# Weight loads four ahead, seven early units, and a later first stage in a fused attention and convolution kernel

## Chip, cores and metric

The kernel runs on one NeuronCore of one Trainium2 chip. The metric is the device time of one execution in microseconds (us), in float32 throughout. Its engines are named as the profile names them: PE (matrix multiply), PEld (its weight loads), DVE (vector), ACT (scalar), POOL (GpSimd) and SP (sync, used here only to issue DMAs).

## The reference

Two layers run one after the other on x of shape (2, 256, 64, 64).

```
# layer 0: global attention, 8 heads of 32 channels over all 4096 positions of an image
m    = resize(mask, bilinear)
q, k, v = 1x1 convolutions of x;  q = q / sqrt(32)
fuse = softmax(q k^T) v
x    = conv1x1(concat[x, fuse], Wf) * m + x * (1 - m)

# layer 1: channel gate, window attention, two grouped 7x7 convolutions
x = x * sigmoid(relu(x ca_w1) ca_w2)
x = x + window_attention(x)          # 8x8 windows, 4 heads of 64
x = channel shuffle(x)
y = relu(bn1(grouped conv7x7(x, sa_w1)))
y = bn2(grouped conv7x7(y, sa_w2))
out = x * sigmoid(y)
```

## The kernel before

**Preparation** (to about 187 us of the span): q, k and v of both images are projected and stored in DRAM, and the mask and the scaled convolution taps are prepared.

**Attention.** The 4096 queries of an image are cut into 8 chunks of 512, so there are 16 chunks (b, c). A chunk has 64 *slots*: 2 groups of 4 heads (g) by 32 key blocks of 128 (m). The slots of all chunks stand in one list, 1024 long, and one loop issues them in that order. In iteration i it issues the scores of slot i + 2 (L633 on PE, exponentials L643 on ACT into a tile e), then the products of slot i (L662 on PE, which read e and v), and the addition of e to the running sum of exponentials (L664 on DVE). The e tiles come from a ring of EB = 8 buffers. A buffer is free again once its product and its addition are done.

**Work put between slots.** `at(delay, action)` runs an action `delay` iterations later. After a chunk's last slot (slot 63 of the first chunk) come, with DN = 8: at + 8 the denominators (matmuls L685, copy L692 to the tile inv); at + 9 their reciprocal (L714 on DVE); at + 10 and + 12 the two halves of `spread` (matmuls L700 with inv as an operand, copy L707 to the tile rd); at + 13 the multiplication of the attention output f by rd (L717 on DVE); and at + 14 the chunk's *stage* is queued. A stage is a generator. The loop advances it by one step in every fourth iteration. Its first step multiplies x and then f by the fusion weights (L732), and its DVE part makes x1 (L744, L746). The following steps are the channel gate (L761, L775), the window attention (L803 to L953), and the storing of the chunk's rows to the DRAM tensor x_s (L979). [...]

**The last part** is the pair of grouped convolutions, `convolve`, also a generator. A *unit* u is 16 of the 256 channels' group work with its own banded weights w_s[u] (896 KB), 16 units in all. `items` lists the pieces of work: the first EARLY units of image 0 alone, the units 2 to EARLY - 1 of image 1 alone, the other units for both images together, and the units 1 and 0 of image 1. Image 1 is complete only when the last chunk's stage has stored its rows. So the first EARLY items run between the steps of that last stage, and fill PE there. For item k, `conv1(k)` is L1045 (56 matmuls), `conv2(k)` is L1069 (56 matmuls), and `gate(k)` multiplies (L1091) and stores the result (L1104). `load_x` (L1024) loads an item's rows from x_s: into four tiles "xe" for k < EARLY and four tiles "xl" after that. `load_w` (L1017) loads a unit's weights. Those of unit 0 have a tile of their own. The others go into the eight e buffers of the attention, in turn, and the order of loads is 1 to 15 and then 1 again. Both kinds of load are issued on SP's queue, where half of the stores stand too (for the early items after the last stage, all stores go to POOL).

The order around the last stage comes from this code:

```
            for _ in range(2):
                load_w(weights.popleft())
            conv1(0)
...
                gate(k, z)
                if xcs or k + 4 < EARLY:
                    load_rows(k + 4)

                if weights and (k < EARLY - 1 or k >= EARLY):
                    load_w(weights.popleft())
```

`more()` (L1110) makes the four xl tiles as soon as the last stage has been issued, and loads the next four items' rows into them.

Of the kernel before, what the change touches and what calls it, by code (L numbers as in the profile page):

```python
# [29 lines left out]
AHEAD = 2  # L30
EB = 8
DN = 8
EARLY = 8
HEADS1, HD1 = 4, 64
WS = 8
NW = W // WS
# [19 lines left out]
def conv_seq_kernel(ctx: ExitStack, tc: tile.TileContext, a, out):  # L56
    nc = tc.nc
# [13 lines left out]
    def psum2(name):  # L71
        return ps["pair"].tile([P, 2, CH], F32, tag="s", name=name)
# [259 lines left out]
    def spread(row, n):  # L332
        f = row.shape[-1]
        return row.rearrange("p u f -> u p f").to_broadcast([NU, n, f])
# [189 lines left out]
    def pipeline(arm, shifted, pools):  # L524
# [23 lines left out]
        stages = deque()  # L548

        def at(delay, action):  # L550
            later.append((now[0] + delay, action))
# [13 lines left out]
        def load_q(b, c):  # L565
            q = qp.tile([P, KC, CH], F32, tag="q", name=f"q{arm}_{b}_{c}")
            nc.sync.dma_start(q, q_s[b, c].rearrange("p (g n) -> p g n", g=KC))
            qts[b, c] = q
# [82 lines left out]
        def products(i):  # L651
            b, c, g, m = slots[i]
            if m == 0:
                acc[0] = avp.tile([P, CH], F32, tag="av", name=f"av{arm}_{i}")
                acc[1] = ep.tile([P, HG, CH], F32, tag="sum", name=f"sum{arm}_{i}", bufs=3)
                totals[b, c, g] = acc[1]
            av, total = acc[0], acc[1]
            e, v = es[i], vts[b, c, g, m // PB]
            start, stop = m == 0, m == NMB - 1
            for j in range(HG):  # L660
                r = slice(32 * j, 32 * j + 32)
                nc.tensor.matmul(av[r, :], v[:, m % PB, r], e[:, j, :], start=start, stop=stop)  # L662
            if m > 0:
                nc.vector.tensor_add(total, first[0] if m == 1 else total, e)  # L664
            e = es.pop(i)
            if start:
                first[0] = e
            if stop:
                if g == 0:
                    fts[b, c] = fp.tile([P, KC, CH], F32, tag="f", name=f"f{arm}_{b}_{c}")  # L670
                f = fts[b, c]
                nc.scalar.copy(f[:, g, :], av)  # L672
                if g == 0:
                    return
                both = [totals.pop((b, c, gg)) for gg in range(KC)]
                inv = fp.tile([P, P], F32, tag="inv", name=f"inv{arm}_{i}")
                rd = fp.tile([P, KC, 4, P], F32, tag="rd", name=f"rd{arm}_{i}")


                def denominators():  # L680
                    s = psum2(f"dn{arm}_{i}")
                    for h in range(HEADS0):
                        for q in range(4):
                            r = slice(32 * q, 32 * q + 32)
                            nc.tensor.matmul(  # L685
                                s[r, 0, 0:P],
                                keysum[:, h].rearrange("p i h -> p (i h)"),
                                both[h // HG][:, h % HG, q * P : (q + 1) * P],
                                start=(h == 0),
                                stop=(h == HEADS0 - 1),  # L690
                            )
                    nc.scalar.copy(inv, s[:, 0, 0:P])  # L692


                def spread(hh):
                    t = psum2(f"rd{arm}_{i}_{hh}")
                    for gg in range(KC):
                        for q in range(2):
                            r = slice(64 * hh + 32 * q, 64 * hh + 32 * q + 32)
                            nc.tensor.matmul(  # L700
                                t[:, q, gg * P : gg * P + P],
                                spread_h[r, gg].rearrange("p j d -> p (j d)"),
                                inv[r, :],
                                start=True,
                                stop=True,
                            )
                    nc.scalar.copy(  # L707
                        rd[:, :, 2 * hh : 2 * hh + 2, :],
                        t[:, :, 0 : KC * P].rearrange("p q (g n) -> p g q n", g=KC),
                    )  # L710


                at(DN, denominators)
                at(DN + 1, lambda: nc.vector.reciprocal(inv, inv))  # L714
                at(DN + 2, lambda: spread(0))
                at(DN + 4, lambda: spread(1))
                at(DN + 5, lambda: nc.vector.tensor_mul(f, f, rd.rearrange("p g q n -> p g (q n)")))  # L717

# [266 lines left out]

        items = [(u, (0,)) for u in range(EARLY)] + [(u, (1,)) for u in range(2, EARLY)]
        items += [(u, (0, 1)) for u in range(EARLY, NU)] + [(1, (1,)), (0, (1,))]
        staged = []  # L990

        def convolve():
# [12 lines left out]
            weights = deque([*range(1, NU), 1])  # L1005
            dst = out.rearrange("b (g i) r w -> b i r g w", i=4)

            def load_w(u):
                if u >= NU:
                    return  # L1010
                n = 2 * 32 * UW
                if u == 0:
                    t = cpool.tile([P, n], F32, name=f"w{arm}{u}")
                else:
                    t = ep.tile([P, HG, CH], F32, tag="e", name=f"w{arm}{u}")
                    t = t.rearrange("p h n -> p (h n)")[:, 0:n]
                nc.sync.dma_start(t, w_s[u])  # L1017
                ws[u] = t

            def load_x(k):  # L1020
                u, images = items[k]
                x = xs[k] = early[k % 4] if k < EARLY else xcs[k % 4]
                for i, b in enumerate(images):
# [5 lines left out]
            def load_rows(k):  # L1029

                while len(xs) < min(k + 1, len(items)) and (
                    staged or B - 1 not in items[len(xs)][1]
                ):
                    load_x(len(xs))
# [53 lines left out]
            def gate(k, z):  # L1088
# [5 lines left out]
                if k == len(items) - 1:  # L1094
                    engines = (nc.scalar, nc.sync)
                elif staged and k < EARLY:
                    engines = (nc.gpsimd,)
# [12 lines left out]
            def more():  # L1110
                if staged and not xcs:

                    for n in range(3):
                        t = ep.tile([P, HG, CH], F32, tag="sum", name=f"xl{arm}{n}", bufs=3)
                        t = t.rearrange("p h n -> p (h n)")[:, 0 : B * nb * UG * WP]
                        xcs.append(t.rearrange("p (n g w) -> p n g w", n=B * nb, g=UG, w=WP))
                    xcs.append(pool.tile([P, B * nb, UG, WP], F32, name=f"xl{arm}3"))
                    load_rows(EARLY + 3)
                return bool(xcs)
# [2 lines left out]
            load_rows(3)  # L1122
            load_w(0)
            pool = yield
            for _ in range(2):
                load_w(weights.popleft())
            conv1(0)
            yield
            for k, (u, images) in enumerate(items):
                while len(xs) <= k + 1 < len(items):  # L1130
                    if not more():
                        yield
                conv1(k + 1)
                yield
                more()
                z = conv2(k)
                yield
                more()
                gate(k, z)
                if xcs or k + 4 < EARLY:  # L1140
                    load_rows(k + 4)

                if weights and (k < EARLY - 1 or k >= EARLY):
                    load_w(weights.popleft())

        def run_later():
# [23 lines left out]
        for i, (b, c, g, m) in enumerate(slots):  # L1170
            now[0] = i
            if (b, c, g, m) == (B - 1, NCHUNK - 1, 0, 0):
                for _ in banded:
                    pass
                conv = convolve()
                next(conv)
            if m % PB == 0:
                load_piece(i // PB + AHEAD)
            if g == KC - 1 and m == 0:
                nxt = (b, c + 1) if c + 1 < NCHUNK else (b + 1, 0)  # L1180
                if nxt[0] < B:
                    load_q(*nxt)
            rest = scores(i + 2) if i + 2 < len(slots) else None
            products(i)
            if rest:
                rest()
            if g == KC - 1 and m == NMB - 1:
                at(DN + 6, lambda b=b, c=c: stages.append(stage(b, c)))
            run_later()
            if i % 5 == 1:  # L1190
                next(banded, None)
            if i % 4 == 0:
                run_stages()
# [102 lines left out]
```

## Time and profile before

| what | value |
|---|---|
| median of 3 runs | 3022.46 us (3018.35 to 3022.87) |
| the profiled execution | 3021.93 us, span 3020.1 us |
| mean granted PE clock | 0.993 |
| PE busy | 2970.8 us, 98% |
| DVE busy | 2503.1 us, 83% |
| ACT busy | 2480.6 us, 82% |
| POOL busy | 267.1 us, 9% |
| attention, first score matmul to last product | 187.4 to 2781 us |
| last part, to the end of the span | 2781 to 3020 us |

Busy shares are averages over stretches with different limits: the attention takes 86% of the span, and what limits the last part has to be read from its own lines. Numbers in the traces are us from the span's start, and a duration of one instruction is in ns. The profiled execution spends 1.8 us outside its span.

### The profile page before, as it was taken

Reading aid. Unit: us, or ns where it says so; the run is one execution under the profiler, and the core shown is the slowest. Engines: PE = TensorE matmul, PEld = TensorE weight load, DVE = VectorE, ACT = ScalarE, POOL = GpSimd, SP = SyncE. Lnnn points to the kernel's source line nnn. Section 1 sums busy time; section 2 is a strip of 40 time slices with the busy share of each in tenths; the row PEclk is TensorE's granted clock in tenths of the full one; section 3 lists DMA queues with packets and bytes.
Section 4 is the critical chain, followed back from the end, with each engine's and each line's share of the span. In section 5 each row is a group of like instructions: output and inputs, shape, how many; then the busy total and the mean of one; then the engine's idle time right before and its main releaser. Section 6 shows DMA issues by size and latency. Waiting matters only on the chain.

```text
span 3020.1 us, 61026 instructions
## 1 busy us (share of the span) xinstructions
PE 2970.8 (98%) x25226; PEld 1017.2 (34%) x25226; DVE 2503.1 (83%) x1348; ACT 2480.6 (82%) x4151; POOL 267.1 (9%) x470
## 2 busy tenths in 40 slices
PE   9999899999999999999999999999999999999897
PEld 3552223223222222222223222323223222323585
DVE  3249989999999999998999999999999998998211
ACT  5569789898989898988989898989898998988333
POOL 8010000000000000000000000000000000000456
PEclk9999999999999999999999999999999999999998
DMA  8544322222142323232222222222323222321564
GB/s 243 196 174 160 107 69 66 69 65 70 52 80 63 79 62 73 66 73 68 67 68 64 71 58 67 62 73 62 80 59 69 71 71 67 104 60 54 163 196 104
DMA packets 224143, 266.03 MB, mean 88 GB/s; under 512 B 113576, under 2 KB 130300, under 8 KB 223600
## 3 DMA queue, kind: packets, MB, share of 16 engines
q1 hardware_dynamic: 200880, 231.47, 26.2%
q0 software_dynamic: 18416, 27.87, 4.4%
q8 instruction: 201, 3.29, 0.5%
q10 hardware_dynamic: 4560, 2.70, 0.3%
q14 instruction: 86, 0.70, 0.1%
HBM read 213.49 MB, written 66.13 MB: 93 GB/s over the span
## 4 chain that ended last, share of the span: by engine, by line
PE 92%; DVE 2%; DMA 2%; POOL 1%; ACT 1%; issue 1%; SPq 0%; ACTq 0%; DVEq 0%; POOLq 0%
PE sa L633 36%; PE ava L662 33%; PE hya L732 4%; PE qka L803 4%; PE vwa L889 2%; PE opa L953 2%; PE v L472 2%; PE q L435 2%; PE k L435 2%; DVE suma L664 1%; POOL out_dram L1104 1%; PE c1a L1045 1%; PE c2a L1069 1%; DMA out_dram<-za 1%; PE dna L685 1%
## 5 line engine op out<-in xcount | busy, mean ns | idle before, releaser
L664 DVE TENSOR_TENSOR suma<-suma,ea 128x2048 f32<-128x2048 f32 x960 | 2199.1, 2291 | 88.7 <-ACT ea L643 2.3
L643 ACT ACTIVATE ea<-sa 128x512 f32<-128x512 f32 (+1 forms) x3072 | 2044.8, 745 | 86.6 <-PE sa L633 39.3
L633 PE MATMUL sa<-qa,ka 32*128 32x512 f32 x8192 | 1191.4, 640 | 1.5 <-ACT vst L480 1.2
L662 PE MATMUL ava<-ea,va 128*32 128x512 f32 x8192 | 1091.6, 605 | 0.3 <-ACT fa L672 0.3
L633 PEld LDWEIGHTS sa<-qa,ka 32*128 32x128 f32 x8192 | 338.0, 183 | 755.4 <-ACT ea L643 688.3
L662 PEld LDWEIGHTS ava<-ea,va 128*32 128x32 f32 x8192 | 161.5, 108 | 779.7 <-issue 752.9
L979 POOL DMA_DIRECT2D xs<-xo x94 | 65.8, 708 | 2552.0 <-DVE xo L964 2551.8
L1104 POOL DMA_DIRECT2D out_dram<-za x210 | 117.9, 569 | 85.0 <-DVE za L1091 61.1
L803 PE MATMUL qka<-ua,qkv_w 128*128 128x512 f32 x256 | 118.4, 605 | 0.0
L664 DVE TENSOR_TENSOR suma<-ea,ea 128x2048 f32<-128x2048 f32 x32 | 73.1, 2284 | 51.3 <-ACT ea L643 51.3
L1091 DVE TENSOR_TENSOR za<-za,xla 128x768 f32<-128x768 f32 (+1 forms) x16 | 21.7, 1359 | 108.0 <-DMA out_dram<-za 57.9
L454 DVE TENSOR_REDUCE top<-sq 128x512 f32<-128x2048 f32 x16 | 36.6, 2286 | 81.3 <-ACT sq L448 81.3
L1069 PE MATMUL c2a<-yca,wa 32*128 32x192 f32 (+1 forms) x1344 | 98.1, 435 | 2.5 <-ACT za L1079 2.5
L740 ACT ACTIVATE ta<-hya,bf 128x512 f32<-128x512 f32 x32 | 20.2, 683 | 96.8 <-PE hya L732 96.8
L1079 ACT ACTIVATE za<-c2a 128x384 f32<-128x384 f32 (+1 forms) x48 | 26.1, 595 | 86.5 <-DMA out_dram<-za 61.4
L1069 PEld LDWEIGHTS c2a<-yca,wa 32*128 32x128 f32 x1344 | 89.6, 315 | 13.1 <-issue 9.8
L858 ACT ACTIVATE ewa<-ewa,mxwa 128x64 f32<-128x64 f32 x256 | 85.2, 346 | 1.5 <-DVE mxwa L849 1.5
L744 DVE TENSOR_TENSOR ta<-ta,mca 128x512 f32<-128x512 f32 x32 | 22.0, 689 | 67.6 <-ACT ta L740 67.6
L816 ACT ACTIVATE qka<-qka,qkv_b 128x512 f32<-128x512 f32 x64 | 40.4, 683 | 41.8 <-PE qka L803 41.6
L803 PEld LDWEIGHTS qka<-ua,qkv_w 128*128 128x128 f32 x256 | 46.0, 189 | 71.3 <-issue 46.1
L435 PE MATMUL q<-x,WqT 128*128 128x512 f32 x128 | 61.3, 624 | 5.6 <-DMA WqT<-in_WqT_dram 5.6
L889 PE MATMUL vwa<-qkv_w,ua 128*128 128x256 f32 x256 | 59.5, 386 | 0.0
(137 smaller groups left out, 1523.5 us busy)
## 6 DMA issues: line engine op xcount, KB each, us to landing
ka<-ks SPq DMA_DIRECT2D x256, 256.0 KB
va<-vs SPq DMA_DIRECT2D x256, 256.0 KB
wa<-ws SPq DMA_DIRECT2D x17, 896.0 KB
ws<-zeros SPq DMA_DIRECT2D x16, 896.0 KB
xs<-xo POOLq DMA_DIRECT2D x78, 140.0 KB, 5.8
xla<-xs SPq DMA_DIRECT2D x24, 420.0 KB
x<-in_x_dram SPq DMA_DIRECT2D x16, 512.0 KB
qs<-qst SPq DMA_DIRECT2D x16, 512.0 KB
```

Of the source, the lines that this page charges most:

```text
L435: nc.tensor.matmul(s[:, g, :], w[:, kc, g * P : (g + 1) * P], rhs, start=(kc == 0), stop=(kc == KC - 1),)
L633: nc.tensor.matmul(heads[j], k[r, cols], q[r, g, :], start=True, stop=not shifted)
L643: nc.scalar.activation(e[:, h, :], tile, AF.Exp, scale=SCALE0)
L662: nc.tensor.matmul(av[r, :], v[:, m % PB, r], e[:, j, :], start=start, stop=stop)
L664: nc.vector.tensor_add(total, first[0] if m == 1 else total, e)
L732: nc.tensor.matmul(s[:, oc, :], wf[:, kc, oc * P : (oc + 1) * P], f[:, kc - KC, :] if half else xw[kc], start=(kc == 0), stop=(kc == 2 * K ...
L803: nc.tensor.matmul(s[:, j, :], wqkv[:, kc, o : o + P], u[:, kc, :], start=(kc == 0), stop=(kc == KC - 1),)
L858: nc.scalar.activation(e[:, n, :], e[:, n, :], AF.Exp, bias=mx[:, n : n + 1], accum_out=rs[:, n : n + 1],)
L889: nc.tensor.matmul(sv[:, t, :], u[:, kc, t * P : (t + 1) * P], wqkv[:, kc, 2 * C : 3 * C], start=(kc == 0), stop=(kc == KC - 1),)
L979: eng.dma_start(x_s[b, n, p + r0 : p + r1].rearrange("r g w -> g r w"), xo[64 * h : 64 * h + 64, oc, r0 - WS * c : r1 - WS * c, :],)
L1069: nc.tensor.matmul(tiles[j // 2][:, j % 2, 0 : n * W], w[r, d], y[r, 0:n, d : d + W], start=(d == 0), stop=(d == KS - 1),)
L1104: engines[stores % len(engines)].dma_start(dst[b, i, r0:r1, UG * u : UG * u + UG, :], z[p + r0 : p + r1, :, nb * m + n, :],)
```

## The change

Two unrelated parts.

In the first chunk only, the two halves of `spread`, the multiplication of f and the start of the stage come EB + 1 = 9 slots later; denominators and reciprocal stay where they were.

In the last part, EARLY goes from 8 to 7. Unit 7 is then done for both images together: 23 items in place of 24. Four units' weights are loaded ahead of the first convolution in place of two, and after each item the next one follows as long as its number is at most 1 + EB = 9, or once the early items are over.

```
-EARLY = 8
+EARLY = 7
...
+                late = EB + 1 if (b, c) == (0, 0) else 0
                 at(DN, denominators)
                 at(DN + 1, lambda: nc.vector.reciprocal(inv, inv))
-                at(DN + 2, lambda: spread(0))
-                at(DN + 4, lambda: spread(1))
-                at(DN + 5, lambda: nc.vector.tensor_mul(f, f, rd.rearrange("p g q n -> p g (q n)")))
+                at(DN + 2 + late, lambda: spread(0))
+                at(DN + 4 + late, lambda: spread(1))
+                at(DN + 5 + late, lambda: nc.vector.tensor_mul(f, f, rd.rearrange("p g q n -> p g (q n)")))
...
-            for _ in range(2):
+            for _ in range(4):
                 load_w(weights.popleft())
...
-                if weights and (k < EARLY - 1 or k >= EARLY):
+                if weights and (weights[0] <= 1 + EB or k >= EARLY):
                     load_w(weights.popleft())
...
-                at(DN + 6, lambda b=b, c=c: stages.append(stage(b, c)))
+                late = EB + 1 if (b, c) == (0, 0) else 0
+                at(DN + 6 + late, lambda b=b, c=c: stages.append(stage(b, c)))
```

## The prediction

> **What bounds the kernel now.** I read the waits of PE over the whole run first, then the order of time around each long wait, then the queue that stands behind it.
>
> ```profile
> PE c1a L1045 <- DMA wa<-ws: 12.5, 3, 9.4
> PE rda L700 <- issue: 9.0, 1, 9.0
> PE q L435 <- DMA WqT<-in_WqT_dram: 5.6, 1, 5.6
> ```
>
> Columns: total us, times, longest. From the first attention slot to the last part PE has one long wait, at L700; all others before the last part that fall into the attention are 1.2 us or less. In the last part it waits three times for weights at L1045. These are the two places that the change touches. In windows of one chunk's length from 378.7 to 2658.8 PE is busy without a gap, 162.86 us per chunk, while DVE is busy for about 151.3 us of it.
>
> The first wait, on PE and on DVE:
>
> ```profile
> 351.20 1.07 PE L662 MATMUL ava<-ea,va 128*32 128x512 f32 x8
> 361.26 1.01 PE L700 MATMUL rda<-inva,spread_h 32*128 32x128 f32 x6 [8.99 <-issue]
> ```
> ```profile
> 343.63 16.67 DVE L664 TENSOR_TENSOR suma<-suma,ea 128x2048 f32<-128x2048 f32 x7
> 360.21 0.94 DVE L714 RECIPROCAL inva<-inva 128x128 f32<-128x128 f32 x1
> ```
>
> Columns: start, duration, then the idle time in brackets. The first chunk has no stage to work on. PE alone needs 2.067 us for a slot, DVE 2.395 us for an addition, so PE runs ahead until the e ring is full (near 298 us) and then keeps DVE's pace. Slot 73's products end at 352.3. The spread needs the reciprocal, which stands on DVE behind the additions up to slot 72 and ends at 361.2: PE waits 9.0 us although the bracket says only "issue". In that time DVE works off all of PE's lead, and from then on PE sets the pace.
>
> The second place, PE and SP's queue:
>
> ```profile
> 2839.46 4.19 PE L1045 MATMUL c1a<-xea,wa 128*32 128x192 f32 x56 [1.84 <-DMA wa<-ws]
> ...
> 2853.20 3.58 PE L1069 MATMUL c2a<-yca,wa 32*128 32x192 f32 x56
> 2866.15 4.62 PE L1045 MATMUL c1a<-xea,wa 128*32 128x192 f32 x56 [9.38 <-DMA wa<-ws]
> 2870.70 3.58 PE L1069 MATMUL c2a<-yca,wa 32*128 32x192 f32 x56
> 2874.20 2.54 PE L1045 MATMUL c1a<-xla,wa 128*32 128x192 f32 x56
> ```
> ```profile
> 2848.76 1.33 SPq L979 DMA_DIRECT2D xs<-xo x2
> 2856.16 2.01 SPq L1024 DMA_DIRECT2D xla<-xs x4
> 2858.22 1.54 SPq L1017 DMA_DIRECT2D wa<-ws x3
> ```
>
> Unit 7's weights are issued behind four row loads, which wait until the last chunk's rows have landed in x_s. The 9.38 us are thus the price of the queue's order. Also, conv1 takes 2.47 us in a row of items, but 4.12 to 4.55 us right after the two longer waits.
>
> **What the Trainium skill says.** "TensorE: Matmul & The Clock Gate" (What's actually happening) has the PE clock fall to half after an idle window of about 3.4 us and return after a busy one. The trace agrees: granted clock 0.50 from 356 to 364 us and from 2862 to 2870, also some 4 us into the work. The same page (Architectural detail) calls DVE strict FIFO; that is the first wait. "DMA: Bandwidth & Descriptors" (Queues, rings and completion order) says that a DMA engine takes the descriptors of one ring in order and alternates between rings by packets. I use it for the first of four row loads landing first; the trace has no landing time for it.
>
> **Part 1, the later spread and stage.** It adds and removes no instruction: 16 matmuls and two copies of `spread`, one DVE multiplication, and the stage's steps with their two loads on SP (next x and mask) and four stores on POOL move by 9, the stage in effect by 8 slots (from 80 to 88, as it starts in every fourth). The loads are for a stage at slot 144, and POOL is idle for hundreds of us there, so the moved DMAs cost nothing.
>
> Slot 82 is where PE now wants the reciprocal. PE passes slot 73 at 352.3; DVE has the reciprocal at 361.2; at 2.067 us per slot PE needs 18.6 us for nine slots. So the old wait goes.
>
> What is late next? With a full ring, L662 of slot i starts 4.2 us after the addition of slot i - 8 ends (319.15 against 314.97 for slot 60). DVE has slot 73's addition done at 363.4, later ones each 2.395 us after. PE: slot 80 at 365.7 by its own pace; from slot 82 by the ring; slot 88 starts at 380.1 + 4.2 = 384.3 and ends at 385.3. The two spread halves (0.65 us each) fit into the 0.33 us that each slot leaves. The stage's first half (x, 3.53 us) ends at 388.8. Its second half needs f, whose multiplication stands on DVE behind slot 85's addition: 363.4 + 12 x 2.395 = 392.1, plus 1.22 = 393.4. **A new wait of about 4.6 us** at L732. Behind it on PE stand the scores of slot 91 on, so ACT waits as well, but DVE still has three additions. For the clock I charge 1.6 us: what the old wait cost after its end (378.65 - 361.26 = 17.4 us for seven slots and the spread, which at full clock are 14.5 + 1.3).
>
> Then 393.4 + 3.53 + 1.6, four slots (8.27) and the gate's first product (1.05) give 407.9. The wait for x1 that stands there is covered: DVE has it at 400.4 + 2.8 = 403.2. Before, the same amount of work was done at 412.66 (first L803, after slot 92) less the second gate product 1.05 = 411.6. **Gain 3.7 us.** It stays, since PE sets the pace thereafter and DVE's end at slot 137 (525.3 before, less at most the 7.4 us it idled in that chunk) is 517.9, ahead of PE's 522.0. Bounds: 5.4 without the clock loss; 7.1, what DVE's unbroken row allows; and 0, if the wait at f is as long as the old one.
>
> **Part 2, weights and units.** Weights 3 and 4 are issued when the additions of their e buffers end, at about 2772 and 2775; SP has nothing else until 2805. So the waits of 1.24 and 1.84 us go, and with the second the slow conv1 (4.12 - 2.47 = 1.65): **4.7 us**, all on PE's path through the stage. Weights 5 to 8 follow the first four gates, one per gate as now, and all stand ahead of the row loads. So the 9.38 us and the slow conv1 after them (4.55 to the next start, less 2.47: 2.1) go, **11.5 us**.
>
> Next late: with EARLY = 7 the eighth conv1 is image 1's unit 2 and needs the first of the row loads. Count from the end of the last L953 (2847.2 now). The rows' load is issued 8.95 us later (2856.16). I take 3.5 us to landing. The skill's fit for one DMA ("DMA: Bandwidth & Descriptors", Anatomy of one DMA: 2.0 us + bytes/436e3) gives the estimate 3.0 for 420 KB; the trace's longest is the 9.9 us in which all four and a weight tile landed. PE meanwhile has conv2, conv1, conv2 = 3.51 + 2.47 + 3.50 = 9.5 us. Wait: 8.95 + 3.5 - 9.5 = 3.0, plus 0.5, since weight 8 now moves while the rows are stored. With 1 us for the clock (nothing to 2.1): **4.5 us come back**; at worst 8.95 + 9.9 - 9.5 + 2 for weight 8 + 2.1 = 13.5; at best, with 3.0 to landing and no more, 2.5.
>
> Unit 7: two single items (2.47 + 3.50 each, 11.94) become one double item (4.74 + 4.89 = 9.63): **2.3 us less**. Later weights keep at least seven items' lead; they reuse buffers whose unit is done. POOL's stores (6.74 us per early item, three instead of four items) end before their z buffer is needed, and the double items leave POOL 2.9 us free in each 9.63, so the end drains as before.
>
> Sum: 4.7 + 11.5 - 4.5 + 2.3 = **14.0 us** (5 to 16). With part 1: 17.7. The profiled execution took 3021.93 (span 3020.1 and 1.8 around it), 0.5 below the median: **3004**.
>
> **Rivals.** *Part 2 alone pays* (the wait at f equals the one removed): 3008. For it: f stands on DVE behind nearly as many additions. Against: the ring limits the backlog. *The row loads take over fully* (all four land together): part 2 gives 5, with part 1 3013. For it: one ring, 0.5 us between issues. *Nothing hangs on these waits* (removed waits reappear elsewhere; the change doesn't do what it says): 3020. Against: PE has no gap between the two places. *All clear* (no clock losses, f in time): 3021.9 - 7.1 - 16 gives 2999. *Slower*: keeping DVE backlogged makes it the bound in every chunk at L700 and L732. Its chunk is 151.3 us busy plus 62 gaps of 0.1, 157; from 162.9 on it decides. At 2 us beyond, 15 chunks cost 30 and the total is 3034. Nothing shows DVE slowed by backlog.
>
> **How the numbers follow.** About 0.2% (6 us) can be told from no change. Forecast, 2999 to 3010: 0.60. Part 2 alone: 0.12, row loads: 0.12, all clear: 0.09, all faster by over 0.2% as 3016 is the border: 0.93. Nothing: 0.04. Slower: 0.03. The range 2997 to 3013 leaves out the last two and some edges.
>
> **What would show it.** After: no wait of 9 us at L700, one of 3 to 6 at L732 in the first chunk with DVE's f as its end; no L1045 wait for wa; one of 2 to 5 for xla at the eighth conv1; 23 pairs of L1045 and L1069 groups, so 112 matmuls fewer; the last L953 some 8 us earlier. Wrong, if L700 or L732 waits come back chunk after chunk, or if the wait for xla is above 10.

## The result, and the profile after

The changed kernel took 3003.48 us (median of 4 runs, 3002.89 to 3005.29) against 3022.66 us before (median of 4 runs, 3018.35 to 3024.31): ratio 0.994, 95% interval 0.9924 to 0.9955. Its profiled execution took 3003.67 us with a span of 3001.9, so the span is 18.2 us shorter. Line numbers after the edit are higher by 3 from L714 on, and in split, best5, best8 and best8_act by one more.

The waits of PE over the whole run, in the changed kernel (total us, times, longest):

```profile
PE q L435 <- DMA WqT<-in_WqT_dram: 5.6, 1, 5.6
PE hya L735 <- DVE fa L720: 4.3, 1, 4.3
PE c1a L1048 <- DMA xla<-xs: 3.8, 1, 3.8
...
PE c2a L1072 <- ACT za L1082: 0.6, 1, 0.6
```

The 9.0 us at L700 and the 12.5 us for weights are gone. Two shorter waits have come: for f in the first chunk's stage, and for the rows of image 1.

The first chunk, PE and then DVE, in order of time (start, duration, idle time before in brackets):

```profile
385.03 3.70 PE L735 MATMUL hya<-xa,WfT 128*128 128x512 f32 x8
393.01 5.40 PE L735 MATMUL hya<-fa,WfT 128*128 128x512 f32 x8 [4.29 <-DVE fa L720]
398.34 1.14 PE L633 MATMUL sa<-qa,ka 32*128 32x512 f32 x8
...
406.61 1.08 PE L764 MATMUL ca1a<-x1a,ca_w 128*64 128x256 f32 x8
```
```profile
359.98 0.95 DVE L717 RECIPROCAL inva<-inva 128x128 f32<-128x128 f32 x1
360.84 30.98 DVE L664 TENSOR_TENSOR suma<-suma,ea 128x2048 f32<-128x2048 f32 x13
391.74 1.22 DVE L720 TENSOR_TENSOR fa<-fa,rda 128x1024 f32<-128x1024 f32 x1
```

DVE now goes through thirteen additions between the reciprocal and f without a pause. PE no longer waits for the reciprocal, but it reaches the stage before DVE reaches f. The second half of L735 takes 5.3 us to the next start in place of 3.53: half clock again (the granted clock was 0.50 from 394 to 396 us).

The last part, PE and SP's queue:

```profile
2832.11 2.54 PE L1048 MATMUL c1a<-xea,wa 128*32 128x192 f32 x56
2834.59 3.70 PE L956 MATMUL opa<-ota,out_w 128*128 128x512 f32 x8
...
2844.18 3.56 PE L1072 MATMUL c2a<-yca,wa 32*128 32x192 f32 x56
2851.57 3.87 PE L1048 MATMUL c1a<-xla,wa 128*32 128x192 f32 x56 [3.83 <-DMA xla<-xs]
2855.37 3.58 PE L1072 MATMUL c2a<-yca,wa 32*128 32x192 f32 x56
```
```profile
2836.41 0.37 SPq L1020 DMA_DIRECT2D wa<-ws x1
2839.77 1.33 SPq L982 DMA_DIRECT2D xs<-xo x2
2847.88 2.00 SPq L1027 DMA_DIRECT2D xla<-xs x4
```

Weight 8 is issued ahead of the last rows' stores, the four row loads follow, and what PE waits for there is rows (xla), not weights.

Where the 18.2 us come from, read off the starts of the same instructions in both profiled executions:

| up to | before | after | earlier by | of it new |
|---|---|---|---|---|
| first conv1 | 2780.79 | 2776.68 | 4.1 | 4.1 |
| start of the last L953 / L956 | 2843.58 | 2834.59 | 9.0 | 4.9 |
| conv2 after the eighth conv1 | 2870.70 | 2855.37 | 15.3 | 6.3 |
| last conv1 | 2993.19 | 2975.46 | 17.7 | 2.4 |
| end of the span | 3020.1 | 3001.9 | 18.2 | 0.5 |

### The profile page after: what moved, and what is told of

It reads as the page before. It is cut to its first block, busy times and chain, and to the rows that moved or that the text cites. A ratio compares the mean times of both kernels' runs of the same rounds, so it can differ in the third digit from the quotient of the medians.

```text
span 3001.9 us, 60791 instructions
## 1 busy us (share of the span) xinstructions
PE 2966.4 (99%) x25114; PEld 1010.4 (34%) x25114; DVE 2501.4 (83%) x1347; ACT 2479.6 (83%) x4147; POOL 263.7 (9%) x464
## 4 chain that ended last, share of the span: by engine, by line
PE 90%; DVE 4%; DMA 2%; POOL 2%; ACT 2%; issue 1%; SPq 0%; ACTq 0%; DVEq 0%; POOLq 0%
PE sa L633 36%; PE ava L662 33%; PE qka L806 4%; PE hya L735 4%; DVE suma L664 3%; PE vwa L892 2%; PE opa L956 2%; PE v L472 2%; PE q L435 2%; POOL out_dram L1107 2%; PE k L435 2%; DMA out_dram<-za 1%; PE dna L685 1%; DVE za L1094 1%; PE sca L840 1%
## 5 line engine op out<-in xcount | busy, mean ns | idle before, releaser
L1094 DVE TENSOR_TENSOR za<-za,xla 128x1536 f32<-128x1536 f32 (+1 forms) x16 | 22.6, 1410 | 110.7 <-ACT za L1088 86.1
L1082 ACT ACTIVATE za<-c2a 128x384 f32<-128x384 f32 (+1 forms) x46 | 25.8, 614 | 84.8 <-DMA out_dram<-za 68.9
L1072 PE MATMUL c2a<-yca,wa 32*128 32x192 f32 (+1 forms) x1288 | 95.1, 438 | 0.6 <-ACT za L1082 0.6
L1072 PEld LDWEIGHTS c2a<-yca,wa 32*128 32x128 f32 x1288 | 86.8, 314 | 11.0 <-issue 9.7
L1048 PE MATMUL c1a<-xla,wa 128*32 128x384 f32 (+1 forms) x896 | 62.5, 429 | 3.8 <-DMA xla<-xs 3.8
```

Of the source, the lines that this page charges most:

```text
L1048: nc.tensor.matmul(s[32 * j : 32 * j + 32, 0 : n * W], w[:, j, d, :], xs[k][:, 0:n, j, d : d + W], start=(d == 0), stop=(d == KS - 1),)
L1072: nc.tensor.matmul(tiles[j // 2][:, j % 2, 0 : n * W], w[r, d], y[r, 0:n, d : d + W], start=(d == 0), stop=(d == KS - 1),)
```

## The experiments

Each kernel was run beside the kernel before on the same chip. Medians of before were 3021.71 us for late_only, part2_only, w4_only and early7_only, 3024.25 for split, rows_rev, w4_both and best8, and 3020.56 for best8_act, late5, best5 and changed. So differences to before are compared, not the times alone. The edits shown are against the changed kernel.

**late_only**: part 1 of the change, nothing else.

```
-EARLY = 7
+EARLY = 8        # and two weights ahead with the old condition
```

> Only the later spread and stage of the first chunk; the last part as in the kernel before. My theory: the wait of 9 us at L700 goes, one of about 4.3 us for f takes its place at the stage's second half, and the time falls by 4 us (3.7 predicted), to about 3018. Rival: the gain belongs to the last part alone and the wait has only moved; then the time stays within 1 us of before.

Measured: 3018.14 us, 3.6 below before (ratio 0.9988, 0.9981 to 0.9994). L735 waits 4.3 us for f, L700 waits no more, and the first conv1 starts at 2776.78, as in the changed kernel. Part 1 gains by itself, and the 3.7 us that the path says lie well inside the interval, which is about 2 to 6 us.

**part2_only**: part 2 alone.

```
-                late = EB + 1 if (b, c) == (0, 0) else 0
+                late = 0
```

> Both edits of the last part, the first chunk as before. My theory: 14 us less than before (about 3008.5), the wait of 9 us at L700 stays, and one of about 4 us for xla stands at the eighth conv1. Rival: the two parts lean on each other (PE arrives otherwise at the last stage); then the two gains do not add up to 18 us.

Measured: 3008.49 us, 13.2 below before (0.9956, 0.9943 to 0.997). L700 keeps its 9.0 us. The two parts add up as far as can be told: 3.6 + 13.2 = 16.8, against 16.9 for the changed kernel in the run named `changed` below, and 19.2 in the first comparison.

**w4_only** and **early7_only** take part 2 apart: only the weights' order, or only the number of early units.

```
# w4_only: late = 0 and
-EARLY = 7
+EARLY = 8
# early7_only: late = 0 and
-            for _ in range(4):
+            for _ in range(2):
-                if weights and (weights[0] <= 1 + EB or k >= EARLY):
+                if weights and (k < EARLY - 1 or k >= EARLY):
```

> Four weights ahead, but EARLY stays 8, first chunk as before. My theory: all three waits for weights go and no wait for rows comes, since unit 7 of image 0 lies between the rows' issue and their first use: 4.7 + 11.5 = 16.2 us less than before, about 3006.5, which is 2 us more than both edits together give. Rival: the seven units are needed to get the gain (the stores of the early items, all on POOL, or the rows hold PE up instead); then the gain is under 12 us.

> Seven early units, but two weights ahead and the old condition, first chunk as before. My theory: the waits of 1.2 and 1.8 us for weights 3 and 5 stay; at the eighth conv1 a wait for rows of about 4 us stands in place of 9.4 for weights; one double item in place of two single ones gives 2.3: about 8.5 us less than before, 3014. Rival: the wait at the eighth conv1 is set by the last stage's rows whatever is loaded; then 2 to 3 us less than before.

w4_only took 3009.33 us: 12.4 below before (0.9957, 0.9944 to 0.9971), not 16.2, though the interval, 9 to 17 us, just reaches that. early7_only took 3011.3: 10.4 below (0.9967, 0.9955 to 0.9979). I expected 8.5, which the interval includes; in its profiled execution the wait of 1.2 us for weight 3 did not come, and the conv1 after the wait for weight 5 ran at full clock (below). In w4_only the waits for weights are gone and none for rows has come, as expected, but PE now waits in a conv2. PE, and then POOL, in the order of time:

```profile
2879.58 0.78 PE L1072 MATMUL c2a<-yca,wa 32*128 32x192 f32 x4
2883.22 4.87 PE L1072 MATMUL c2a<-yca,wa 32*128 32x192 f32 x52 [2.85 <-ACT za L1082]
```
```profile
2849.78 8.47 POOL L1107 DMA_DIRECT2D out_dram<-za x15 [3.40 <-DVE za L1094]
2858.65 2.13 POOL L1107 DMA_DIRECT2D out_dram<-za x4 [0.40 <-DMA out_dram<-za]
2861.30 2.95 POOL L1107 DMA_DIRECT2D out_dram<-za x5 [0.52 <-DMA out_dram<-za]
2865.04 11.63 POOL L1107 DMA_DIRECT2D out_dram<-za x21 [0.79 <-DMA out_dram<-za]
2877.28 5.13 POOL L1107 DMA_DIRECT2D out_dram<-za x9 [0.61 <-issue]
```

With EARLY = 8 four items' stores are POOL's alone, 48 DMAs. POOL is at them, and at six of the next item, from 2849.8 to 2882.4 with hardly a gap, and the tanh that needs a z buffer (ACT L1082) waits for it. From the start of that conv2 to the next conv1 PE takes 8.4 us in place of 3.5. So my claim that seven units would be the worse choice with four weights ahead fell: what they cost in rows (5 us), eight units cost in stores. By time the two choices, part2_only and w4_only, can't be told apart. early7_only shows the other half: the wait of 1.8 us for weight 5 stays, and the eighth conv1 waits 3.0 us for rows in place of 9.4 for weights.

**w4_both** and **best8** give the early stores two queues, to take POOL's limit away; best8 has the split of the next experiment as well.

```
-                elif staged and k < EARLY:
-                    engines = (nc.gpsimd,)
```

> Four weights ahead with EARLY = 8 and the first chunk as before, like the run w4_only, but the stores of the early items after the last stage go to POOL and SP in turn in place of POOL alone. My theory: w4_only lost its 2.9 us wait at L1072 and some 2 us of half clock to POOL, which needs 6.74 us for an item's stores while PE brings one each 5.97; with two queues these go: 4 to 5 us below w4_only, 3005. Rival: the stores wait for DMA capacity, not for POOL's issue; then it stays at 3009.

> All that should help: four weights ahead, EARLY = 8, early stores on two queues, and in the first chunk spread and f 5 slots later, the stage 9. My theory: the gains of w4_both (16) and of the split (7) add up to about 23 us below before: 2999, the fastest. Rival: the units' merging (2.3 us) outweighs the wait for rows, so it comes out no faster than the changed kernel with the split.

w4_both took 3012.35 us, 11.9 below its before (0.9963, 0.9949 to 0.9977): no gain over w4_only. The wait at L1072 is still 3 us, only earlier. PE, then POOL and SP:

```profile
2863.67 4.34 PE L1072 MATMUL c2a<-yca,wa 32*128 32x192 f32 x52 [2.97 <-ACT za L1082]
```
```profile
2848.65 3.43 POOL L1105 DMA_DIRECT2D out_dram<-za x6 [3.40 <-DVE za L1094]
2852.45 2.91 SPq L1027 DMA_DIRECT2D xla<-xs x4
2855.47 3.31 SPq L1105 DMA_DIRECT2D out_dram<-za x6
```

SP's six stores of the fifth item stand behind the four row loads, which wait for the last chunk's rows. So they are issued 6.8 us after POOL's six stores of the same item, and ACT's next write to that buffer waits for stores ("DMA out_dram<-za", 8.6 us). Landing was slow there too: POOL's stores issued between 2854 and 2860 us took 4.8 us to land (median), in the last part of before 2.7. My theory that issue on POOL was all that stood in the way fell. best8 took 3002.79 (0.9929, 0.9915 to 0.9942), with a wait of 2.9 us at this conv2 (L1073 there), not 2999: no faster than split, as the rival had it.

**best8_act** tries the other queue, ACT's, for the second half of these stores.

```
-                    engines = (nc.gpsimd,)
+                    engines = (nc.gpsimd, nc.scalar)
```

> The kernel of the run best8 (four weights ahead, EARLY = 8, split), but the early stores after the last stage go to POOL and ACT in turn in place of POOL and SP. My theory: in w4_both and best8 the 3 us wait at L1072 came from stores that stood on SP's ring behind four row loads; on ACT's ring they do not, so the wait goes and the time falls 3 to 5 us below best8, about 25 us below before. Rival: the stores compete with the row loads for the DMA engines whatever their ring; then the wait at L1072 stays at 2 us or more and the time is within 1 us of best8.

Measured: 3007.51 us, 13.1 below before (0.9955, 0.9942 to 0.9969), worse than best8. ACT, with its queue, and PE:

```profile
2840.43 9.42 ACTq L1108 DMA_DIRECT2D out_dram<-za x6
2849.89 0.42 ACT L1057 ACTIVATE yca<-c1a,cbias 128x192 f32<-128x192 f32 x1 [10.49 <-DMA xla<-xs]
...
2852.98 2.51 ACTq L1108 DMA_DIRECT2D out_dram<-za x6
```
```profile
2850.37 4.25 PE L1049 MATMUL c1a<-xea,wa 128*32 128x192 f32 x56 [6.79 <-ACT yca L1057]
```

The wait at L1072 (here L1073) fell to 0.3 us, but ACT was at six stores for 9.4 us while the rows were stored and loaded again, against 2.5 us for six a little later. The relu behind them (L1057) came late and PE waited 6.8 us for it. Neither of my two theories foresaw that. It is not that a store takes ACT long to issue. One took 0.3 to 0.6 us, as the first line here shows (min/median/max in ns); the other two lines are pieces of the chain that ended the wait:

```profile
L1108 ACTq DMA_DIRECT2D out_dram<-za x6: 315/328/608, 2840.4 to 2849.5; - x6
```
```profile
2844.45 5.06 DMA xla<-xs
...
2849.53 0.32 ACTq L1108
```

The rest of the 9.4 us is waiting. In the trace's operands the DMAs of SP and ACT share eight semaphores that report their landing (numbers 100 to 107), and a store of ACT is issued only when the DMA that had its semaphore before has landed. For the third store that was a store of the last chunk's rows on SP, landed at 2843.32; for the fourth, fifth and sixth the first three row loads, landed at 2846.95, 2848.20 and 2849.51. Each store was issued 0.02 us after that. So the row loads held ACT's stores up from another queue, as they held up SP's stores in w4_both by standing ahead of them.

**split** and **late5** ask what sets the new wait for f. In split, spread and f come 5 slots later and the stage 9; in late5 all come 5 later.

```
# split
+                late = 5 if (b, c) == (0, 0) else 0
                 at(DN + 2 + late, lambda: spread(0))
# late5, in both places
-                late = EB + 1 if (b, c) == (0, 0) else 0
+                late = 5 if (b, c) == (0, 0) else 0
```

> The changed kernel, but spread and the multiplication of f in the first chunk come 5 slots later in place of 9, the stage still 9. My theory: f is then ready at about 383.5 us, 5 us before the stage's second half wants it, so the wait of 4.3 us at L735 and its clock loss go; about 2 us come back as a wait for x1 at L764 and, a chunk later, at L700. 2 to 3.5 us below the changed kernel: 3000.5. Rival: any stall that goes here returns in full within the next chunk, since DVE is the bound there; no change, 3003.5.

> The changed kernel with spread, f and stage of the first chunk all 5 slots later in place of 9. My theory: the wait for f is set by the distance of f and stage on a full ring, not by how late both are, so it stays at 4.3 us, now at slot 84; the time is within 1.5 us of the changed kernel, rather below. Rival: less delay leaves DVE more backlog to finish and the wait grows towards the old 9 us: 3 us or more above the changed kernel.

split took 3001.02 us, 23.2 below its before (0.9925, 0.9911 to 0.9938). Its first chunk on PE:

```profile
388.55 3.60 PE L736 MATMUL hya<-fa,WfT 128*128 128x512 f32 x8
401.41 0.65 PE L765 MATMUL ca1a<-x1a,ca_w 128*64 128x256 f32 x4 [0.99 <-DVE x1a L750]
402.64 0.65 PE L765 MATMUL ca1a<-x1a,ca_w 128*64 128x256 f32 x4 [0.58 <-DVE x1a L750]
```

No wait for f; 1.6 us here for x1; no wait at L700 one chunk later. The first conv1 starts at 2772.24, 4.4 us before that of the changed kernel. That is more than the 2 to 3.5 us I expected: the 4.3 us of wait and 1.8 us of clock are gone, and only the 1.6 us came back. late5 took 3002.22, 1.5 below `changed` with overlapping runs, so by time it can't be told from it. It waits 3.7 us for f at 383.56: less delay did not bring the old wait back. In these three runs the distance between f's place in DVE's queue and the stage is what counts.

**rows_rev** reverses the four row loads, to see whether the order on one queue decides which lands first.

```
-                    load_rows(EARLY + 3)
+                    for n in range(3, -1, -1):
+                        load_x(EARLY + n)
```

> The changed kernel, but the four row loads after the last stage are issued in reverse, so that the eighth conv1's rows are the last of the four. My theory: loads of one queue land in order, each 1.1 us of transfer apart, so the wait for xla grows from 3.8 to about 7 us and the slow conv1 after it by up to 0.9: 3.5 to 4 us above the changed kernel, 3007. Rival: the four share the DMA engines and land together, or the rows' stores set the landing; then no change.

Measured: 3010.43 us, 13.8 below its before (0.9953, 0.994 to 0.9967), where the changed kernel is 16.9 to 19.2 below. PE:

```profile
2857.35 4.72 PE L1048 MATMUL c1a<-xla,wa 128*32 128x192 f32 x56 [8.26 <-DMA xla<-xs]
```

The wait grew by 4.4 us. Part of that is a later issue: counted from the issue of the four loads (2849.70 us here), PE went on after 7.65 us in place of 3.69, so three places in the queue cost 4.0 us, 1.3 us per load in place of my 1.1. The landings in best8_act, 1.25 and 1.31 us apart, agree. Loads of one queue landed in their order here; "all four land together" is out.

**best5** is split with five weights ahead and none at the fourth gate; **changed** is the changed kernel on the same chip.

```
-            for _ in range(4):
+            for _ in range(5):
-                if weights and (weights[0] <= 1 + EB or k >= EARLY):
+                if weights and (weights[0] <= EB or k >= EARLY):
```

> The kernel of the run split, with five weights ahead and no weight issued at the fourth gate, so that weight 8 no longer moves while the last chunk's rows are stored. My theory: the rows land about 0.7 us earlier, and with the shorter wait for xla less is lost to the clock: 0.7 to 2 us below split, about 22 to 25 below before. Rival: the stores' own time sets the landing; then it equals split.

> The changed kernel once more, to stand beside the other three on one chip: about 18.5 us below before, with waits of 4.3 us at L735 and about 4 us at L1048 for xla.

`changed` took 3003.67 us, 16.9 below before (0.9941, 0.9927 to 0.9955); its wait for rows was 2.8 us, where I expected about 4. best5 took 2999.84, 20.7 below (0.9928, 0.9914 to 0.9941), the lowest median of all here; its slowest run, 3000.66, is under the fastest of `changed`, 3002.44. Against split, which ran beside another before, it can't be told apart by time. In best5 the row loads are issued 8.74 us after the last L957 ends, in split 10.06, in the changed kernel 9.66. That looks like a delay of 1 us by weight 8, but in `changed`, which moves weight 8 as well, it is 8.67 us. So the spread between executions covers it, and a delay by weight 8 is not shown. The shorter wait for xla brought little, as the next section says.

## Why the prediction was right, point by point

- **The old wait is a queue of additions.** Right. It went with the reciprocal left where it was on DVE, only PE's use of it came later; late_only shows it alone.
- **Part 1, 3.7 us.** 4.1 measured, of which 0.2 is an earlier start of the attention (187.17 against 187.40). Wait for f 4.29 us (4.6 predicted), clock loss 1.8 (1.6), end of the gate's first product 407.6 (407.9).
- **Part 2, the stage's waits, 4.7 us.** 4.9 measured. But part of that was luck: 1.65 of it is the slow conv1 after a wait of 1.84 us, and early7_only and late_only have waits of 1.80 and 1.50 us in that place and conv1 at full speed after them. The wait for weight 3 varies as well: 1.24 us in before, 1.00 in late_only, none in early7_only.
- **Part 2, 11.5 away and 4.5 back.** 6.3 net where I had 7.0. The rows' loads were issued 9.66 us after the last L956 (8.95 + 0.5 predicted) and PE went on 3.7 us after their issue (3.5); wait 3.83, clock loss 1.3 (3.5 and 1.0). The 3.0 us from the Trainium skill ("DMA: Bandwidth & Descriptors", Anatomy of one DMA) is a fit for DMAs that GpSimd issues, and the row loads are SP's, so that estimate was borrowed; the 3.7 us here decide. The 0.5 us for weight 8 are not shown: in `changed` the rows were issued 8.67 us after the last L956, and the wait was 2.77 us with a loss of 1.65. With part2_only (2.54 and 1.5) the three executions give back 4.0 to 5.2 us, around the 4.5 predicted.
- **Unit 7, 2.3 us.** 2.4 measured.
- **The end.** I let it drain as before. PE's last conv1 is 17.7 us earlier, and so is the last multiplication (L1091, now L1094: 3011.77 and 2994.05), which in both kernels is held up by the stores of the z buffers. PE's last wait at L1072, 2.5 us before and 0.6 after, is not on that path: from 2972 us on, the chain that ended last has no PE in it in either kernel. The span is 0.5 us shorter than these 17.7 us explain; what these 0.5 us are is not shown.
- **The sum.** The terms give 17.7, which happens to be PE's gain in this pair of executions; by the medians it is 19.2 and, in `changed`, 16.9. From the profiled 3021.93 it gives 3004.2, and with the 0.5 to the median 3004.7, where I wrote 3004.
- **The rivals.** "Part 2 alone pays" is refuted by late_only, the row loads' full takeover by the wait of 3.83 us and, as to landing together, by rows_rev. Nothing was slower, and in the changed kernel PE waits for DVE nowhere in the attention after the first chunk's stage.

The size of a clock loss was the weakest term. The end of a wait in conv1, and what that conv1 then lost (time to the next start, less 2.47 us):

| run | wait, us | lost, us |
|---|---|---|
| late_only | 1.50 | 0.0 |
| early7_only | 1.80 | 0.0 |
| before | 1.84 | 1.65 |
| best5 | 2.60 | 2.2 |
| `changed` | 2.77 | 1.65 |
| changed kernel | 3.83 | 1.3 |
| split | 4.53 | 1.3 |
| before | 9.38 | 2.1 |

The granted clock in 2 us windows, before and then early7_only, around the wait of 1.8 us (PE, PEld, DVE, ACT, POOL busy, PEclk, DMA share, GB/s):

```profile
2840.00:2842.00 2.00, 2.00 (x31) 1.78 (x27) 0.00 (x0) 0.00 (x0) 2.00 (x5) 0.50 0.34 69
```
```profile
2840.00:2842.00 2.00, 2.00 (x38) 1.49 (x31) 0.00 (x0) 0.42 (x1) 2.00 (x5) 1.00 0.30 59
```

Nearly the same wait, once with half clock behind it and once without. The Trainium skill ("TensorE: Matmul & The Clock Gate", What's actually happening) calls the activity window of about 3.4 us free-running, so it is not aligned with a wait. That would let equal waits end differently. But the page has the half clock follow an idle window of about 3.4 us, and here a wait of 1.84 us was enough once; the measurement decides. That the alignment is the cause here is an inference.

## What to carry to other kernels

When an engine stalls because its operand stands behind a backlog on another engine's queue, delaying the consumer removes the stall, but then look for the next operand produced on the same queue: its distance to its own consumer decides, and delaying both together keeps that wait (late5), while delaying only the last consumer removes it (split). Loads that wait for nothing belong ahead of loads that wait for something on the same queue; then count what each item between still covers, stores included. When a DMA seems slow to issue, look at the duration of each single issue first: it may be waiting for a load of another queue (best8_act). Price a PE wait as its length plus a clock loss, in these runs between nothing and 2.2 us and not in proportion to the wait.

## What the runs showed of the hardware that I had not expected

The row loads, 1.7 MB in four DMAs, held up stores on both hardware queues tried: on SP by standing ahead of them, on ACT because a store waits for the semaphore that a row load still had. ACT was at six stores for 9.4 us, of which one took 0.6 us at most, and its relu came late. A shorter wait of PE can lose more to the clock than a longer one, and then saves little: 2.60 us plus 2.2 of half clock in best5, against 3.83 plus 1.3 in the changed kernel.
